# Moving background steps of a scan kernel by one or two scans, and clearing its padded images one at a time from a row of zeros

## The chip, the core and the metric

The kernel runs on one core of one Trainium2 chip. The metric is the device time of one execution in microseconds. A core has TensorE (PE, matmuls into PSUM), VectorE (DVE), ScalarE (ACT), GpSimd (POOL) and SyncE (SP), which here issues all DMAs. Each engine takes its instructions in program order and waits on semaphores for the others.

## What is computed

Eight images of 64 channels and 128 x 128 pixels, in float32, go one after the other through an adaptive filter and a block with two bidirectional state-space layers:

```python
# layer 0: a 3x3 filter with weights of its own for every pixel
h = leaky(conv3x3(x, w1)); w_lp = softmax(conv1x1(h, w2))      # 9 weights a pixel
x = x + sum_k shift_k(x) * (delta_k - w_lp_k)
# layer 1, on each image
x_norm = layernorm(x); seq = layernorm(tokens(x_norm)); res = seq    # 16384 tokens
for i in range(2):
    xz = rmsnorm(seq) @ in_proj                                 # x and z, 128 channels
    seq = seq + (mamba(x, z, forward) + mamba(x, z, backward)) @ out_proj
x_mamba = conv3x3(rmsnorm(seq), resconv) + res
x = x + depthwise3x3(conv1x1(x_norm)) * x_mamba
g1, g2 = split(depthwise3x3(conv1x1(layernorm(x), ffn_in)))     # 2 x 170 channels
x = x + conv1x1(gelu(g1) * g2, ffn_out)

# mamba, one direction
xc = silu(causal_conv1d(x)); dt_r, Bm, Cm = xc @ xproj
dt = softplus(dt_r @ dtproj + bias)
h[t] = exp(dt[t] * A) * h[t-1] + dt[t] * xc[t] * Bm[t]          # 128 channels x 16 states
y = (sum_n h * Cm + D * xc) * silu(z)
```

## The kernel before

**Scans.** The recurrence runs on DVE as a scan instruction along 1024 tokens, with 128 of the 128 x 16 (channel, state) pairs on the partitions. So a chunk of 1024 tokens takes 16 scans. An image has 16 chunks, two layers and two directions, 1024 scans; eight images have 8192. For scan `u` of a chunk ACT makes the decay `w` = exp(dt A) in one of two PSUM buffers (`decay`, L993), POOL makes the drive `bu` for two scans at once (`drive`, L985, three buffers), DVE scans (L1011, or L1013 in the backward direction), DVE (L1035) or POOL (L1032) multiplies by C (`product`), ACT keeps the last state (`keep`, L1025), and PE sums over the states (`collect`, L1051).

**The order of the work** is written out by hand. Nothing is issued at once: `at(time, phase, fn)` puts a step into a table, with the number of the scan beside which it is to be issued as its time and one of six phases in that scan (FEED, SCAN, MID, PROD, DECAY, REST). At the end the table is sorted and issued; that is the order of each engine's queue. The scheduler adds no order of its own, only the waits. Times below 0 come ahead of the first scan. Steps of the same time and phase stand in the order in which they were put in: the chunks' first, then image by image those of the front, of mix and of FFN.

**A chunk** prepares itself over the 32 scans ahead of its own (`Chunk.plan`): load of normed tokens, convolution, silu at -21, dt at -18 and -17 (`step`, L904), softplus at -14, B and C at -16, the store of dt to DRAM (`store_dt`, L938), then `dtx` on POOL (L941), which overwrites dt by dt * xc and so must wait for that store, the store of du, and the loads that spread both over the states (L952, L963). The second direction of a layer adds at its end, in the next chunk's scans, output projection, residual and rmsnorm: `means` on PE (L399), `means_out` on ACT (L405), `root` on POOL (L408, a power of -0.5), `spread` back over the channels on PE (L414), `normed` on DVE (L1097).

**Background.** Beside the scans of one image run, spread over the table: the *front* of the next image (layer 0, layer norms, the pointwise part of the depthwise branch; 16 pieces of 1024 pixels, one every 24 scans; `hidden` L442, `hidden_out` L446, `weighted` L498, `scaled` L523, `third_norm` L555), and of the image before *mix* (16 pieces, one every 13 scans: two 3x3 convolutions on PE, L638, `add_h` L651, `times` on DVE L658, `plus` on POOL L661, a layer norm) and *FFN* (16 pieces, one every 24 scans: three groups of convolutions on PE, L740 and L746; `first_out` L753; `gelus` on ACT, L757 and L759; `rest_times` L762; `times` L765; `project`; `add`; `store`). The front of the first image runs mostly ahead of the first scan; mix and FFN of the last image end after the last scan.

**PSUM** tiles that matter: chunk steps share one bank ("mm"), background steps two ("acc" and "bg"), the decays have two buffers ("w"). A step that needs one of these waits until the last reader of the tile before is through.

**Images in DRAM.** The 3x3 convolutions read windows out of five padded images (`x_img`, `xm_img`, `xn_img`, two `dw_img`), 64 rows of 131 x 130 floats each, whose rims must be zero. Before, ahead of all background, one tile of 64 x 17030 zeros is filled by DVE (L335) and stored into each of the five (L337); then pad columns of three token arrays are stored (L339, L340). `copy_x` (L618) copies an image of x into `x_img` in 16 pieces.

**SP** issues some 25,700 DMAs, all on one hardware queue; an issue that waits holds all behind it.

Of the kernel before, what the change touches and what calls it, by code (L numbers as in the profile page):

```python
# [8 lines left out]
F32 = mybir.dt.float32  # L9
# [7 lines left out]
C = 64  # L17
# [22 lines left out]
FRONT_STEP, MIX_STEP, FFN_STEP = 24, 13, 24  # L40
FRONT_AT, MIX_AT, FFN_AT = 594, 992, 1204

SILU, SOFTPLUS, GELU = 11, 18, 11

FIRST_FRONT_AT = -198
LAST_MIX_STEP, LAST_MIX_AT, LAST_FFN_STEP, LAST_FFN_AT = 16, 826, 12, 1084
# [9 lines left out]
def kernel(ctx: ExitStack, tc: tile.TileContext, a: dict, out: bass.AP):  # L56
# [20 lines left out]
    def dram(shape, name):  # L77
        return dramp.tile(shape, F32, tag=name, name=name + "_dram")


# [234 lines left out]

    def image(name):

        return dram([C, PW * PW + PW], name)

    def pixels(img):  # L320
        return img[:, 0 : PW * PW].rearrange("c (r w) -> c r w", w=PW)

    x_img, xm_img, xn_img = image("x"), image("xm"), image("xn")
    dw_img = [image(f"dw{i}") for i in range(2)]
    x1_dram = [dram([NCH, P, N], f"x1{i}") for i in range(2)]

# [5 lines left out]
    yf_dram = dram([NT, DI, T], "yf")  # L332
    with tc.tile_pool(name="zeros", bufs=1) as zp:
        zero = zp.tile([C, PW * PW + PW], F32, tag="zero", name="zero")
        nc.vector.memset(zero, 0.0)  # L335
        for img in (x_img, xm_img, xn_img, *dw_img):
            nc.sync.dma_start(img, zero)  # L337
        for t in (*hn0_dram, hn1_dram):
            nc.sync.dma_start(t[:, 0:PAD], zero[:, 0:PAD])  # L339
            nc.sync.dma_start(t[:, PAD + NT * T :], zero[:, 0:PAD])  # L340

# [85 lines left out]
    class Front:  # L427
# [134 lines left out]
        def plan(self, a):  # L562
# [3 lines left out]
            for i in range(3):  # L566
                at(b + 1 + i, REST, self.hidden, i)
            at(b + 4, DECAY, self.hidden_out)
            at(b + 21, REST, self.logits)
# [58 lines left out]
    class Mix(Front):  # L628
# [40 lines left out]
        def plan(self, a):  # L669
            n1 = self.n1  # L670
            at(a - 5, REST, self.load_conv, dw_img[self.p], "dww")
            at(a - 4, REST, self.load_conv, xm_img, "xmw")
            at(a - 1, REST, self.load_h)
            for i in range(3):
                at(a + i, REST, self.conv, 0, "dww", i)
                at(a + 3 + i, REST, self.conv, 1, "xmw", i)
            at(a + 3, DECAY, self.branch_out)
            at(a + 2, REST, self.load_x1)
            at(a + 5, REST, self.add_h)
            at(a + 7, DECAY, self.times)  # L680
            at(a + 7, REST, self.plus)
            at(a + 9, REST, self.store_x2)
            at(a + 9, REST, self.centered, bg_tile, "x1")
            at(a + 10, DECAY, self.centered_out)
            at(a + 11, REST, lambda: n1.means(bg_tile, self.sq))
            at(a + 12, DECAY, n1.means_out)
            at(a + 12, REST, n1.root)
            at(a + 15, REST, n1.spread, bg_tile)
            at(a + 16, DECAY, self.scaled, n1)
            at(a + 16, DECAY, self.norm)  # L690
            at(a + 16, REST, self.store_rows, xn_img, "hc")

# [6 lines left out]
    class Ffn:  # L699
# [54 lines left out]

        def gelus(self):
            for h in range(2):
                nc.scalar.activation(self.ga[h], self.ga[h], AF.Gelu)  # L757
            self.gt = tmp("gt")
            nc.scalar.activation(self.gt, self.rest[0], AF.Gelu)  # L759

# [31 lines left out]
        def plan(self, a):  # L792
            early = 12 if self.alone else 0
            at(a - 4 - early, REST, self.load, 0)
            at(a - 3 - early, REST, self.load, 1)

            if self.alone:
                groups = ((0, 0, self.first_out, 2), (3, 2, None, 0), (6, 1, self.times, 9))
                gelus, out = 5, 12
            else:  # L800
                groups = ((0, 0, self.first_out, 5), (6, 2, None, 0), (13, 1, self.times, 18))
                gelus, out = GELU, 20
            for t, g, end, to in groups:
                for i in range(4):
                    at(a + t + (0 if self.alone else i), REST, self.conv, g, i)
                for h in range(2 if end else 0):
                    at(a + to, DECAY, end, h)
            at(a + gelus, REST, self.gelus)
            at(a + gelus + 2, PROD, self.rest_times)
            at(a + out - 5, REST, self.load_x2)  # L810
            at(a + out, REST, self.project)
            at(a + out + 2, DECAY, self.add)
            at(a + out + 2, REST, self.store)
# [15 lines left out]
    class Chunk:  # L829
# [282 lines left out]
        def plan(self):  # L1112
# [17 lines left out]
            at(b - 14, REST, self.store_bc)  # L1130
            at(b - 12, REST, self.store_dt)
            at(b - 11, FEED, self.dtx)
# [37 lines left out]
            at(b + 12, FEED, lambda: n.means(mm_tile, self.sq))  # L1170
            at(b + 12, DECAY, n.means_out)
            at(b + 13, REST, n.root)
            at(b + 17, FEED, n.spread, mm_tile)
# [6 lines left out]
    for i, c in enumerate(chunks):  # L1180
        c.prev = chunks[i - 1] if i else None
        c.plan()
    for b in range(B):
        a, last = IMAGE * b, b == B - 1
# [36 lines left out]
```

## Time and profile before

| | |
|---|---|
| median of three runs | 30239.16 us (30228.46 to 30248.67) |
| the profiled execution | 30193.53 us; its span 30191.6 us |
| busy in the span | PE 24336.3, DVE 27115.8, ACT 18589.4, POOL 27650.2 us |
| first scan starts, last scan ends | 680.5 us, 29577.9 us |
| DMA | 6617 MB, 219 GB/s over the span |
| one scan, L1011 w | 2345 ns, 2677 of them |
| one product on DVE (L1035), on POOL (L1032) | 1225 ns, 2358 ns |
| one drive for two scans on POOL (L985) | 4534 ns |
| one decay on ACT (L993) | 1118 ns |

In the profile's lines a group is named by line, engine, operation and out<-in with the program's tile names. A wait is written as the waiting engine and instruction, an arrow, and what ended the wait. "SPq" is SP's issue of a DMA; the DMA itself lands later. In a timeline the columns are start in us, duration in us, engine, line, operation and tiles, how many instructions are merged, and in brackets the idle time of the engine before it with what ended it. A PE of which the profile says that it is busy needn't be at its peak.

### The profile page before, as it was taken

The numbers are of one execution on the slowest core, as the hardware profiler recorded it, in microseconds if no ns is written. First come the engines' busy times: TensorE is split into PE (matmuls) and PEld (weight loads), VectorE is DVE, ScalarE is ACT, GpSimd is POOL, SyncE is SP. The second block draws the span as 40 slices with busy tenths as digits, with TensorE's granted clock in tenths as the row PEclk, the third lists the DMA queues.
The fourth block names the chain that finished last, engine by engine and source line by source line (L and its number), as shares of the span: only waits on it lengthen the run. The fifth ranks groups of instructions, "written<-read, shape, count | busy, mean of one in ns | idle before, by whom it ended". The sixth has DMA issues, their size and how long they took to land. (4 is left out here: it accounts for less than half of the span.)

```text
span 30191.6 us, 307698 instructions
## 1 busy us (share of the span) xinstructions
PE 24336.3 (81%) x96344; PEld 8057.2 (27%) x96344; DVE 27115.8 (90%) x17258; ACT 18589.4 (62%) x28316; POOL 27650.2 (92%) x8732
## 2 busy tenths in 40 slices
PE   6766888878888788887888788887888878888589
PEld 2211232223222232222322223222232223322123
DVE  2999999999899998999999999999999999999992
ACT  2666666666666665666666666666666666666661
POOL 1999999999999999999999999999999999999991
PEclk8877889989899888988989889898899988999789
DMA  3676676766777667776777767677677766767672
GB/s 92 211 237 217 220 230 227 238 213 221 229 232 233 214 222 229 234 232 213 228 228 234 225 215 229 228 237 224 216 227 231 237 217 223 231 229 233 215 237 76
DMA packets 2488415, 6617.27 MB, mean 219 GB/s; under 512 B 417862, under 2 KB 680342, under 8 KB 2483830
## 3 DMA queue, kind: packets, MB, share of 16 engines
q1 hardware_dynamic: 2486774, 6597.59, 67.3%
q8 instruction: 761, 12.47, 0.2%
q14 instruction: 880, 7.21, 0.1%
HBM read 5363.40 MB, written 1266.10 MB: 220 GB/s over the span
## 5 line engine op out<-in xcount | busy, mean ns | idle before, releaser
L985 POOL TENSOR_TENSOR bu<-dup,bp 128x2048 f32<-128x2048 f32 x4096 | 18558.9, 4534 | 215.1 <-DVE w L1011 74.1
L993 ACT ACTIVATE w<-dtp,a_neg 128x1024 f32<-128x1024 f32 x8192 | 9158.4, 1118 | 394.7 <-DVE hs L1011 170.4
L1035 DVE TENSOR_TENSOR hs<-w,cp 128x1024 f32<-128x1024 f32 x5360 | 6565.0, 1225 | 333.8 <-DMA cp<-bc_dram 111.3
L1032 POOL TENSOR_TENSOR hs<-hs,cp 128x1024 f32<-128x1024 f32 x2832 | 6679.1, 2358 | 131.7 <-ACT state L1025 88.4
L1011 DVE TENSOR_TENSOR_SCAN w<-w,state,bu 128x1024 f32<-128x1024 f32 x2677 | 6278.0, 2345 | 297.3 <-ACT w L993 296.7
L1013 DVE TENSOR_TENSOR_SCAN w<-w,state,bu 128x1024 f32<-128x1024 f32 x2683 | 6289.9, 2344 | 262.1 <-ACT w L993 261.9
L1051 PE MATMUL y<-hs,sel_y 128*32 128x512 f32 x32768 | 5182.2, 705 | 103.0 <-POOL hs L1032 100.9
L1025 ACT COPY state<-w 128x1 f32<-128x1 f32 x5360 | 835.2, 156 | 5403.4 <-DVE hs L1035 5355.9
L1013 DVE TENSOR_TENSOR_SCAN hs<-w,state,bu 128x1024 f32<-128x1024 f32 x1413 | 3310.4, 2343 | 260.5 <-ACT state L1025 95.2
L1011 DVE TENSOR_TENSOR_SCAN hs<-w,state,bu 128x1024 f32<-128x1024 f32 x1419 | 3324.3, 2343 | 113.2 <-ACT w L993 54.8
L1044 PE MATMUL y<-xc,dskip 128*64 128x512 f32 x4096 | 1609.4, 853 | 1574.3 <-ACT yv L1068 1117.7
L863 PE MATMUL xp<-hn,wx 128*128 128x512 f32 x4096 | 2280.2, 684 | 719.3 <-ACT xc L869 603.5
L740 PE MATMUL fp<-fw,bgw 128*128 128x512 f32 (+1 forms) x6144 | 2288.4, 627 | 129.9 <-ACT ga L753 67.7
L408 POOL TENSOR_TENSOR r<-r,neg_half 128x8 f32<-128x8 f32 x768 | 1258.2, 1642 | 569.1 <-ACT r L405 494.7
L1051 PEld LDWEIGHTS y<-hs,sel_y 128*32 128x32 f32 x32768 | 751.7, 118 | 3801.2 <-issue 2601.8
L941 POOL TENSOR_TENSOR dt<-dt,xc 128x1024 f32<-128x1024 f32 x512 | 1208.6, 2361 | 568.9 <-DMA dt_dram<-dt 504.4
L1025 ACT COPY state<-hs 128x1 f32<-128x1 f32 x2832 | 538.5, 190 | 1701.2 <-DVE hs L1013 886.4
L904 PE MATMUL dp<-xc,wdt 128*128 128x512 f32 x2048 | 1229.1, 684 | 432.8 <-ACT dt L911 401.0
L746 PE MATMUL fp<-fw,bgw 64*128 64x512 f32 (+1 forms) x6144 | 1511.3, 612 | 0.0
L993 ACT ACT_TABLE_LOAD x1134 | 1454.9, 1283 | 20.6 <-DMA dtp<-dt_dram 0.6
L504 PE MATMUL acc<-t,ident 128*128 128x512 f32 x2304 | 1370.3, 679 | 0.0
L414 PE MATMUL rb<-ident,r 128*64 128x128 f32 x12288 | 959.3, 302 | 461.9 <-ACT state L1025 226.2
(184 smaller groups left out, 26678.6 us busy)
## 6 DMA issues: line engine op xcount, KB each, us to landing
bp<-bc_dram SPq DMA_DIRECT2D x4096, 256.0 KB, 3.8
dup<-du_dram SPq DMA_DIRECT2D x4096, 256.0 KB, 5.0
dtp<-dt_dram SPq DMA_DIRECT2D x4096, 256.0 KB, 5.1
cp<-bc_dram SPq DMA_DIRECT2D x4096, 256.0 KB, 4.8
hn<-hn_dram SPq DMA_DIRECT2D x1024, 256.5 KB, 4.4
dt_dram<-dt SPq DMA_DIRECT2D x512, 512.0 KB, 4.5
du_dram<-dt SPq DMA_DIRECT2D x512, 512.0 KB, 2.6
yf_dram<-yv SPq DMA_DIRECT2D x512, 256.0 KB, 3.5
```

The costliest lines, as they stand in the source:

```text
L740: nc.tensor.matmul(o, wpair[:, i, g, m], self.win[h][:, i : i + ROWS, 0:W], start=(i == 0), stop=False)
L746: nc.tensor.matmul(o, wlast[rows, i, g, m], self.win[h][rows, i : i + ROWS, lo : W + lo], start=False, stop=(i == 2),)
L863: nc.tensor.matmul(self.xp[h], wx[:, self.l, self.d, i, :], self.hn2[:, s.start + 2 * i : s.stop + 2 * i], start=(i == 0), stop=(i == 1),)
L985: nc.gpsimd.tensor_tensor(bu, self.dup[self.pairs[k][1]], self.over_pair("bp", k), ALU.mult)
L993: nc.scalar.activation(w, self.dtp[gp][:, i, :], AF.Exp, scale=a_neg[:, self.l, self.d, g, j : j + 1])
L1011: nc.vector.tensor_tensor_scan(to, w, bu, s0, ALU.mult, ALU.add)
L1013: nc.vector.tensor_tensor_scan(to[:, ::-1], w[:, ::-1], bu[:, ::-1], s0, ALU.mult, ALU.add)
L1025: nc.scalar.copy(self.column(u), h[:, T - 1 : T] if self.d == 0 else h[:, 0:1])
L1032: nc.gpsimd.tensor_tensor(hs, hs, c, ALU.mult)
L1035: nc.vector.tensor_tensor(hs, w, c, ALU.mult)
L1044: nc.tensor.matmul(self.y[C * h : C * h + C, :], dskip[:, self.l, self.d, C * gp : C * gp + C], self.xc[:, s], start=True, stop=False,)
L1051: nc.tensor.matmul(self.y[lo : lo + 32, :], sel_y, hs[:, i, s], start=False, stop=(k % 4 == 3))
```

## The change

- Five images are no longer cleared from a tile of 64 x 17030 zeros ahead of everything. A constant row of 130 zeros on 64 partitions is filled, and `clear` stores it 131 times over into one image with one DMA. `x_img` is cleared first of all, ahead of the loads of weights; `dw_img[0]` at the start of the first front (step -199), `xm_img` at step 64, `xn_img` at 128, `dw_img[1]` at 192, each behind the chunks' and ahead of the background's steps of its time and phase.
- The front starts one scan earlier (593 for 594, -199 for -198), and `hidden_out` stands two scans later in it.
- In mix, `times`, `plus` and all that follows come one scan later.
- In FFN, the gelu of the rest group is issued first of three, its product `rest_times` comes a scan earlier (in phase DECAY of +12 instead of PROD of +13), the third group of convolutions and its `times` one scan later, and the projection one scan earlier.
- In the chunks, the store of dt is issued one scan earlier, and `means_out` and `root` of the closing norm one scan later.

No arithmetic changes. The number of instructions is the same on each engine, apart from waits: 25,719 DMAs as before. Which products POOL takes stays as it was.

```diff
-FRONT_AT, MIX_AT, FFN_AT = 594, 992, 1204
+FRONT_AT, MIX_AT, FFN_AT = 593, 992, 1204
-FIRST_FRONT_AT = -198
+FIRST_FRONT_AT = -199
...
+    def clear(img):
+        nc.sync.dma_start(
+            img.rearrange("c (r w) -> c r w", w=PW),
+            zero.rearrange("c (o w) -> c o w", o=1).to_broadcast([C, PW + 1, PW]),
+        )
+
+    x_img, xm_img, xn_img = image("x"), image("xm"), image("xn")
+    dw_img = [image(f"dw{i}") for i in range(2)]
+    zero = const([C, PW], "zero")
+    nc.vector.memset(zero, 0.0)
+    clear(x_img)
...
-    with tc.tile_pool(name="zeros", bufs=1) as zp:
-        zero = zp.tile([C, PW * PW + PW], F32, tag="zero", name="zero")
-        nc.vector.memset(zero, 0.0)
-        for img in (x_img, xm_img, xn_img, *dw_img):
-            nc.sync.dma_start(img, zero)
-        for t in (*hn0_dram, hn1_dram):
-            nc.sync.dma_start(t[:, 0:PAD], zero[:, 0:PAD])
-            nc.sync.dma_start(t[:, PAD + NT * T :], zero[:, 0:PAD])
+    for t in (*hn0_dram, hn1_dram):
+        nc.sync.dma_start(t[:, 0:PAD], zero[:, 0:PAD])
+        nc.sync.dma_start(t[:, PAD + NT * T :], zero[:, 0:PAD])
...
-            at(b + 4, DECAY, self.hidden_out)
+            at(b + 6, DECAY, self.hidden_out)
...
-            at(a + 7, DECAY, self.times)
-            at(a + 7, REST, self.plus)
-            at(a + 9, REST, self.store_x2)
-            at(a + 9, REST, self.centered, bg_tile, "x1")
-            at(a + 10, DECAY, self.centered_out)
...
+            at(a + 8, DECAY, self.times)
+            at(a + 8, REST, self.plus)
+            at(a + 10, REST, self.store_x2)
+            at(a + 10, REST, self.centered, bg_tile, "x1")
+            at(a + 11, DECAY, self.centered_out)
...
         def gelus(self):
+            self.gt = tmp("gt")
+            nc.scalar.activation(self.gt, self.rest[0], AF.Gelu)
             for h in range(2):
                 nc.scalar.activation(self.ga[h], self.ga[h], AF.Gelu)
-            self.gt = tmp("gt")
-            nc.scalar.activation(self.gt, self.rest[0], AF.Gelu)
...
-                groups = ((0, 0, self.first_out, 5), (6, 2, None, 0), (13, 1, self.times, 18))
-                gelus, out = GELU, 20
+                groups = ((0, 0, self.first_out, 5), (6, 2, None, 0), (14, 1, self.times, 19))
+                gelus, out = GELU, 19
...
-            at(a + gelus + 2, PROD, self.rest_times)
+            at(a + gelus + 1, DECAY, self.rest_times)
...
-            at(b - 12, REST, self.store_dt)
+            at(b - 13, REST, self.store_dt)
...
-            at(b + 12, DECAY, n.means_out)
-            at(b + 13, REST, n.root)
+            at(b + 13, DECAY, n.means_out)
+            at(b + 14, REST, n.root)
...
+    for t, img in ((FIRST_FRONT_AT, dw_img[0]), (64, xm_img), (128, xn_img), (192, dw_img[1])):
+        at(t, REST, clear, img)
```

(In mix, all later steps of `plan` move by the same one scan.)

More of the change, by code (lines that the diff above doesn't have):

```diff
@@ L78, in dram, with image, pixels @@
         return dramp.tile(shape, F32, tag=name, name=name + "_dram")
+    def image(name):
+        return dram([C, PW * PW + PW], name)
+    def pixels(img):
+        return img[:, 0 : PW * PW].rearrange("c (r w) -> c r w", w=PW)
+    def clear(img):
[8 more added lines that the diff above has]
+    clear(x_img)
     ident = const([P, P], "ident")
@@ L313 @@
                 nc.vector.tensor_scalar(dskip[:, l, d, :], ident, dp, None, ALU.mult)
[L316 to L324, printed above, removed]
     x1_dram = [dram([NCH, P, N], f"x1{i}") for i in range(2)]
@@ L679, in plan @@
             at(a + 5, REST, self.add_h)
-            at(a + 7, DECAY, self.times)
-            at(a + 7, REST, self.plus)
-            at(a + 9, REST, self.store_x2)
-            at(a + 9, REST, self.centered, bg_tile, "x1")
-            at(a + 10, DECAY, self.centered_out)
[L685 to L691, printed above, removed]
+            at(a + 8, DECAY, self.times)
[3 more added lines that the diff above has]
+            at(a + 11, DECAY, self.centered_out)
+            at(a + 12, REST, lambda: n1.means(bg_tile, self.sq))
+            at(a + 13, DECAY, n1.means_out)
+            at(a + 13, REST, n1.root)
+            at(a + 16, REST, n1.spread, bg_tile)
+            at(a + 17, DECAY, self.scaled, n1)
+            at(a + 17, DECAY, self.norm)
+            at(a + 17, REST, self.store_rows, xn_img, "hc")
     def plan_mix(b, a, step):
```

## The prediction

> **What bounds the kernel now.** I read the page first, then the stretches of time, then what VectorE (DVE) and GpSimd (POOL) wait for while scans run, then the timeline of the opening.
>
> ```profile
> span 30191.6 us, 307698 instructions
> ## 1 busy us (share of the span) xinstructions
> PE 24336.3 (81%) x96344; PEld 8057.2 (27%) x96344; DVE 27115.8 (90%) x17258; ACT 18589.4 (62%) x28316; POOL 27650.2 (92%) x8732
> ```
>
> Two engines are full at once. The stretches part the span in three: the opening, 0 to 680.5 us (the first scan), in which DVE works only some 135 us; 680 to 29578 us, the 8192 scans, with DVE busy 26940 and POOL 27575 of 28898 us; then a tail of 613 us in which PE is busy 576. One step of the plan (one scan) is 28898 / 8192 = 3.53 us. So three kinds of time can be won: the opening, DVE's idle 1958 us among the scans (6.8%), and POOL's idle 1323 us as far as DVE waits for POOL. PE's tail stays.
>
> The opening, by its timeline:
>
> ```profile
> 102.34 14.25 DVE L335 MEMSET zero<- 64x17030 f32 x1 [3.70 <-issue]
> 116.66 0.66 SPq L337 DMA_DIRECT2D x_dram<-zero  x1
> ...
> 139.86 0.45 SPq L340 DMA_DIRECT2D hn_dram<-zero  x1
> 161.16 0.45 SPq L339 DMA_DIRECT2D hn_dram<-zero  x1
> 182.43 0.45 SPq L340 DMA_DIRECT2D hn_dram<-zero  x1
> 203.74 49.73 SPq L618 DMA_DIRECT2D x_dram<-in_x  x16
> 253.52 2.90 SPq L382 DMA_DIRECT2D xa<-x_dram  x2
> ...
> 269.00 9.82 PE L442 MATMUL hp<-xa,bgw 128*64 128x512 f32 x18 [170.78 <-DMA xa<-x_dram]
> ```
>
> The weights are ready at 98.6 us; the first matmul of the front starts at 269.0, after 170.78 us of waiting. Between lie five images' zeros. The issues at 139.86, 161.16, 182.43 and 203.74 are 21.3 us apart: each stands until one more image (4.36 MB) is written, since an issue on SP waits for the DMA eight before it.
>
> What DVE, then POOL, waits for from 750 to 29500 us (us in total, times, longest):
>
> ```profile
> DVE w L1011 <- ACT w L993: 296.2, 262, 3.9
> DVE w L1013 <- ACT w L993: 261.9, 185, 4.9
> DVE dwv L658 <- PE cv L651: 208.9, 87, 4.7
> DVE hc L523 <- PE rb L414: 187.1, 129, 4.1
> DVE hn L1097 <- PE rb L414: 123.5, 95, 7.9
> ...
> DVE hn L555 <- PE rb L414: 102.9, 69, 5.3
> ```
> ```profile
> POOL dt L941 <- DMA dt_dram<-dt: 504.4, 212, 9.8
> POOL r L408 <- ACT r L405: 278.9, 160, 4.4
> ```
>
> POOL's longest wait, for the store of dt, is in part a wait of an engine that is ahead: DVE stood only 35.4 us for POOL's bu in that stretch.
>
> [...] pad stores of 12 bytes a row, issued behind the images, landed after 94.3 us. [...] from 680 to 29500 us packets of 4096 bytes took 188 ns on average, those of 4104 bytes 279. [...] The trace has the load (1283 ns, 1.28 us) and 0.02 us behind it [...].
>
> **The change, part by part.** Plus is a loss.
>
> 1. *Opening.* Gone from the path: the 14.25 us memset and the wait for five images. Added: one clear of x at the very start, 64 x 131 = 8384 pieces of 520 bytes. The nearest row is the 512-byte packets into these images, 38 ns: 8384 x 38 ns / 16 engines = 20 us. The upper bound adds the 91 ns that 4104 bytes cost over 4096: 129 ns, 68 us. I take 25 us. It isn't free: SP's eighth DMA after it waits for it, so instead of at 15.2 us the first weights (w1n) are issued at about 25 + 17 issues x 0.62 = 36 us, and the whole preparation is some 20 us later. SP is through with its weights at 84 us now, so at 104; six pad stores make 107. From the second copy of x (225.1 us) to the first matmul now pass 43.9 us; so the matmul starts at 151 instead of 269: **-118** (-138 if the preparation isn't held, -75 at 68 us a clear). The clear of dw0 lies after the second load of xa, in today's time 7.6 us ahead of the matmul; the load of xb behind it is used 26 us after that. Some 28 us are covered, so 0; at 68 us it costs 40.
>
> 2. *The three clears at steps 64, 128, 192.* Each closes the queue for 25 us = 7 steps, in the first front. The store of dt lands then at about step 8 of the chunk instead of 5, and POOL stands at L941 some 12 us, of which its lead over the scans takes a part: 8 us each, **+24** (+5 to +160).
>
> 3. *Mix, from `times` on one step later.* PE is late with the convolution; L658 waits 2.4 us on average, at most 4.7; a step is 3.53. Nearly all 209 us of it go. Next late are the decay w from ScalarE (ACT; 1.4 us a chunk in these stretches) and rb. DVE is the fuller engine's follower here (idle 5.4 us of a chunk's 56.9, POOL 2.95), so I take two thirds: **-135** (-70 to -209). `plus`, the stores and the norm move along at the same distances. In the tail nothing moves, as no scan sets the pace.
>
> 4. *A PSUM clash that goes.* Last front chunk and first mix chunk both ask for the one "bg" tile at step 1001: rb (L414) stood 4.60 us for ACT's hc (L520) at 11441 us, and DVE 5.16 us for it at L555. The front now asks at 1000, mix at 1002: seven images x 5.2 = 36, I take **-30** (-36 to 0).
>
> 5. *Front one step earlier otherwise.* The three `hidden` groups leave PE at chunk steps 10 to 12 instead of 11 to 13, so dp at 14 finds PE free (ACT waits 518 us for dp in all); other meetings turn for the worse. **-30** (-120 to +60). `hidden_out` two steps later frees ACT's queue in front of first_norm: in the opening both were ready within 1 us (376.1 and 377.1 us), so 0.
>
> 6. *Store of dt one step earlier.* In the 188 chunks where POOL waits over 1 us at L941, the store was issued a median 3.3 us after softplus had ended, with SP busy otherwise; now it is next. Some 400 of 504 us of POOL's wait go. But who waits for L941 is PE's y for 23.9 us, rb for 3.0 and DVE for 0.4; with a share of DVE's waits for rb I take **-50** (-150 to +20).
>
> 7. *Means and root of the chunk's norm one step later.* ACT's r comes clear of the silu burst; POOL's 279 us at L408 shrink, but two steps remain to the use. **-10** (-40 to +40).
>
> 8. *FFN.* rest_times (L762) goes from step +13 to +12, the gelu it needs (0.58 us) from third to first. Over the 112 gelus beside scans the table load ends 1.35 us (median) after DVE is through with step +12, so the gelu's result comes 1.9 to 2.2 us after; DVE stands 2.1 us and works 0.69 ahead of scan +13. Now, rest_times follows scan +13, and scan +14 then stands 1.43 us for its decay. New: 2.1 + 0.69 + 3.55 (scan and product) = 6.4 us to scan +14; now 5.7. That is +0.7 x 100 = +70 (0 to +258). The convolution at +14 then no longer stands for rest_times (51 us on PE), but in every second FFN chunk its last part meets dp at chunk step 14. Together **+70**.
>
> Sum: -118 + 24 - 135 - 30 - 30 - 50 - 10 + 70 = -279. The profiled execution took 30193.53 us, its span 30191.6 and 1.9 around it; it would take 29914. It lies 46 us (0.15%) below the median of the runs, 30239.16, so the median falls to **29960 us** (0.9% less). One measurement tells 0.2%, about 60 us, from no change.
>
> **Rivals.** (a) *The gelu's wait isn't given back:* DVE stands 2.3 us at each of 112 rest_times and scan +14 is as late as ever: +258 instead of +70, and the steady gains are gone: 30239 - 279 + 188 = 30148. For it: the burst on ACT (three gelus, two loads, 4.3 us) isn't shorter. Against: DVE would have stood 1.43 us anyway. (b) *POOL is the bound* (it is busier, 95.4% against 93.2%): its waits at L941 and L408 then count, 300 instead of 60: 29720. Against: DVE hardly waits for bu. (c) *SP is held by the early store.* It now stands for softplus in nearly every chunk; queued behind it are load_hn, which PE needs four steps later, and the windows. If that makes each of 512 chunks 0.8 us later, +410, and part 6 falls away: 30239 - 229 + 410 = 30420, slower. It decides from 0.57 us a chunk. Against: a load lands in 4.4 us and has 14. (d) *The clears don't do what they say:* at 68 us each, parts 1 and 2 give +125 instead of -94: 30180.
>
> **Chances.** Forecast 0.53, (a) 0.18, (b) 0.13, (c) 0.08, (d) 0.08. The forecast's own range is 29850 to 30070. The range of 8 in 10 reaches to (a) and most of the way to (b): 29750 to 30160. Faster by over 0.2%: nearly all of the forecast, (b), most of (a), half of (d): 0.81; within 0.2%: 0.10; slower 0.09.
>
> **What would show it.** First hp matmul near 150 us and first scan near 562 instead of 680.5; L658's wait for cv below 60 us; L555's wait at mix start gone; POOL's L941 below 150; DVE idle ahead of L762 about 200 us beside scans, and less ahead of scan +14; three stalls of 5 to 15 us at the steps 64, 128 and 192. I am wrong if the first matmul stays above 200 us, or if DVE's waits among the scans (1958 us) don't shrink by at least 100.

## The result, and the profile after

| | before | after |
|---|---|---|
| median, us | 30234.28 (30228.46 to 30248.67) | 29968.85 (29955.96 to 29988.73) |
| ratio | | 0.9912, 95% interval 0.9895 to 0.9929 |
| the profiled execution, us | 30193.53 | 29956.31 |
| first hp matmul, us | 269.0 | 160.6 |
| first scan starts, us | 680.5 | 579.7 |
| from the first scan's start to the last one's end, us | 28897.4 | 28757.6 |
| from there to the end, us | 613.7 | 617.1 |

The time fell by 265 us (0.88%); 29960 had been forecast. Two profiled executions differ by 237 us, since the one of before lay 41 us under its median and the one of after 13: of these 237 the opening gives 101 and the scans 140, and the tail takes 3.

I call the third last row "the scans" below. It is worked out from the starts of DVE's scans in the trace, and so are the lengths of chunks (from the first scan of one chunk to the first of the next).

**The page.** Both engines did the same work as before in less time:

```profile
span 29954.4 us, 307972 instructions
## 1 busy us (share of the span) xinstructions
PE 24257.7 (81%) x96344; PEld 8093.1 (27%) x96344; DVE 27086.6 (90%) x17258; ACT 18533.8 (62%) x28316; POOL 27661.8 (92%) x8732
```

**The opening**, SP's timeline first, then PE's and DVE's:

```profile
1.38 0.57 SPq L89 DMA_DIRECT2D x_dram<-zero  x1
2.00 23.91 SPq L160 DMA_DIRECT2D v_norm_w<-in_L_conv_norm_w  x1
...
41.97 0.31 SPq L216 DMA_DIRECT2D w1n<-in_L_conv_w  x1
...
112.74 31.03 SPq L624 DMA_DIRECT2D x_dram<-in_x  x16
143.88 3.00 SPq L388 DMA_DIRECT2D xa<-x_dram  x2
...
153.87 0.55 SPq L89 DMA_DIRECT2D dw_dram<-zero  x1
```
```profile
160.61 10.44 PE L448 MATMUL hp<-xa,bgw 128*64 128x512 f32 x18 [35.49 <-DMA xa<-x_dram]
```
```profile
192.98 0.69 DVE L504 TENSOR_TENSOR t<-xb,wb 128x512 f32<-128x512 f32 x1 [16.91 <-DMA xa<-x_dram]
```

The wait of PE shrank from 170.78 to 35.49 us. But the clear of x holds SP at the very next issue, for 23.91 us, and the first weights (w1n) go out at 42.0 us instead of 15.2. (The eighth issue behind the clear stands once more, until the clear has landed at 32.7 us, as the eighth behind the first image of zeros did before, until 139.86 us; so SP would have stood that long without the first stand.) The last line is the clear of dw0 at work: the first `weighted` comes 32.4 us after the first hp matmul instead of 26.1.

**The clear at step 64**, on SP, then PE, ACT, DVE and POOL:

```profile
812.88 0.60 SPq L89 DMA_DIRECT2D xm_dram<-zero  x1
816.28 22.15 SPq L517 DMA_DIRECT2D x_dram<-x  x1
838.53 1.21 SPq L566 DMA_DIRECT2D hn_dram<-hn  x2
839.79 1.04 SPq L940 DMA_DIRECT2D bc_dram<-bc  x2
840.93 0.38 SPq L944 DMA_DIRECT2D dt_dram<-dt  x1
841.41 5.49 SPq L859 DMA_DIRECT2D hn<-hn_dram  x2
```
```profile
850.59 3.75 PE L869 MATMUL xp<-hn,wx 128*128 128x512 f32 x4 [19.28 <-DMA hn<-hn_dram]
```
```profile
854.37 0.69 ACT L875 ACTIVATE xc<-xp,cbias 128x512 f32<-128x512 f32 x1 [16.43 <-PE xp L869]
```
```profile
858.57 2.35 DVE L1017 TENSOR_TENSOR_SCAN hs<-w,state,bu 128x1024 f32<-128x1024 f32 x1 [16.21 <-ACT w L999]
```
```profile
848.86 2.35 POOL L947 TENSOR_TENSOR dt<-dt,xc 128x1024 f32<-128x1024 f32 x1 [19.09 <-DMA dt_dram<-dt]
```

Read them from the top down. SP stands 22 us, so the load of hn for a chunk to come is issued only at 841.4, and its second half only at 846.4, when the clear has landed; PE stands at its convolution for hn, ACT at the eviction xc of that convolution, the decay w is queued behind xc on ACT, and DVE's scan stands for w. Beside this runs a second path: the store of dt was held too, POOL stands 19.09 us for it, and its drive for the same scan is ready at 855.7 us, only 2.8 ahead of w (at step 192 the two are 0.5 us apart). So without the delay of hn this scan would still have stood about 13 us, an estimate from these two times. The chunks of the three clears took 75.1, 73.9 and 69.8 us instead of 55.3, 55.3 and 50.5, together 57.7 more.

**What DVE, then POOL, waits for**, 700 to 29250 us (the window shown of before was 750 to 29500; each leaves out some 70 us of scans at the start and 80 at the end):

```profile
DVE w L1017 <- ACT w L999: 340.3, 298, 3.2
DVE w L1019 <- ACT w L999: 313.5, 193, 3.2
DVE hc L529 <- PE rb L420: 209.9, 112, 4.5
DVE gt L768 <- ACT gt L763: 171.8, 107, 2.2
DVE hn L1103 <- PE rb L420: 133.3, 78, 3.7
DVE hn L561 <- PE rb L420: 123.4, 63, 14.4
```
```profile
POOL bu L991 <- DVE w L1019: 421.4, 274, 2.6
POOL dt L947 <- DMA dt_dram<-dt: 221.4, 118, 20.4
POOL hs L1038 <- ACT state L1031: 131.0, 149, 3.9
POOL bu L991 <- DVE w L1017: 116.3, 90, 2.9
POOL r L414 <- ACT r L411: 101.6, 101, 2.6
```

The wait of `times` for cv (208.9 us before) has gone from the list, the wait of `rest_times` for the gelu is new. POOL waits less for the store of dt and for r, and much longer for DVE to leave bu's buffers (537.7 instead of 146.3 us): POOL is ahead of DVE.

### The profile page after: what moved, and what is told of

It reads as the page before. It is cut to its first block, busy times and chain, and to the rows that moved or that the text cites. A ratio compares the mean times of both kernels' runs of the same rounds, so it can differ in the third digit from the quotient of the medians.

```text
span 29954.4 us, 307972 instructions
## 1 busy us (share of the span) xinstructions
PE 24257.7 (81%) x96344; PEld 8093.1 (27%) x96344; DVE 27086.6 (90%) x17258; ACT 18533.8 (62%) x28316; POOL 27661.8 (92%) x8732
## 3 DMA queue, kind: packets, MB, share of 16 engines
q1 hardware_dynamic: 2528054, 6597.59, 68.4%
## 5 line engine op out<-in xcount | busy, mean ns | idle before, releaser
L1038 POOL TENSOR_TENSOR hs<-hs,cp 128x1024 f32<-128x1024 f32 x2832 | 6685.3, 2361 | 197.9 <-ACT state L1031 133.3
L1041 DVE TENSOR_TENSOR hs<-w,cp 128x1024 f32<-128x1024 f32 x5360 | 6564.9, 1225 | 310.9 <-DMA cp<-bc_dram 77.6
L1017 DVE TENSOR_TENSOR_SCAN w<-w,state,bu 128x1024 f32<-128x1024 f32 x2677 | 6280.9, 2346 | 346.5 <-ACT w L999 345.9
L1019 DVE TENSOR_TENSOR_SCAN w<-w,state,bu 128x1024 f32<-128x1024 f32 x2683 | 6291.0, 2345 | 314.1 <-ACT w L999 313.5
L1017 DVE TENSOR_TENSOR_SCAN hs<-w,state,bu 128x1024 f32<-128x1024 f32 x1419 | 3321.3, 2341 | 86.4 <-ACT w L999 36.9
L1019 DVE TENSOR_TENSOR_SCAN hs<-w,state,bu 128x1024 f32<-128x1024 f32 x1413 | 3307.7, 2341 | 52.8 <-ACT w L999 34.7
L746 PE MATMUL fp<-fw,bgw 128*128 128x512 f32 (+1 forms) x6144 | 2353.9, 638 | 64.7 <-ACT ga L759 63.5
L875 ACT ACTIVATE xc<-xp,cbias 128x512 f32<-128x512 f32 x1024 | 697.2, 681 | 1415.1 <-PE xp L869 1414.7
```

What stands on the lines that cost most here:

```text
L746: nc.tensor.matmul(o, wpair[:, i, g, m], self.win[h][:, i : i + ROWS, 0:W], start=(i == 0), stop=False)
L1017: nc.vector.tensor_tensor_scan(to, w, bu, s0, ALU.mult, ALU.add)
L1019: nc.vector.tensor_tensor_scan(to[:, ::-1], w[:, ::-1], bu[:, ::-1], s0, ALU.mult, ALU.add)
L1038: nc.gpsimd.tensor_tensor(hs, hs, c, ALU.mult)
L1041: nc.vector.tensor_tensor(hs, w, c, ALU.mult)
```

## The experiments

Each run is built on the changed kernel, but for the first, which is built on the one before. The kernel before ran on the same chip beside each group of four; its median was 30239 us beside runs 1 to 4, 30224 beside 5 to 8 and 30275 beside 9 to 12. So medians of different groups are comparable to some 40 us only, and I give the scans too, which come from one profiled execution each. The executions of a run lie up to 60 us apart. "Against after" is the difference from 29968.85, and from 28757.6.

| run | median, us | ratio to before, 95% | against after | scans | against after |
|---|---|---|---|---|---|
| before + clears alone | 30166.11 | 0.9978 (0.9969 to 0.9987) | | 28958.3 | |
| FFN back | 29916.83 | 0.9897 (0.9884 to 0.9911) | -52 | 28689.8 | -68 |
| store of dt back | 30109.86 | 0.9962 (0.9948 to 0.9976) | +141 | 28911.0 | +153 |
| mix back | 30068.49 | 0.9944 (0.9932 to 0.9957) | +100 | 28852.6 | +95 |
| front and hidden_out back | 29888.60 | 0.9887 (0.9872 to 0.9902) | -80 | 28713.0 | -45 |
| norm's steps back | 29958.96 | 0.9911 (0.9896 to 0.9926) | -10 | 28754.2 | -3 |
| rest_times alone back | 29938.98 | 0.9903 (0.9888 to 0.9918) | -30 | 28747.1 | -11 |
| clears in eighths | 29876.10 | 0.9881 (0.9865 to 0.9898) | -93 | 28693.3 | -64 |
| own du, store of dt back | 29910.60 | 0.9885 (0.9870 to 0.9900) | -58 | 28705.4 | -52 |
| own du | 29947.62 | 0.9895 (0.9881 to 0.9910) | -21 | 28722.3 | -35 |
| hidden_out alone back | 29887.77 | 0.9875 (0.9858 to 0.9891) | -81 | 28677.1 | -81 |
| eighths, FFN and front back | 29763.47 | 0.9834 (0.9819 to 0.9849) | -205 | 28582.5 | -175 |

**1. The clears alone.** The kernel before with the part of the diff from `image` and `clear` to the pad stores, and the line that plans the four clears; no step is moved.

> The kernel before with the new clears alone (one row of zeros, x cleared at the start, dw0 at -198, xm, xn and dw1 at 64, 128 and 192); every step of mix, FFN, front, norm and the store of dt where it was. Theory: the clears bring the whole of the opening's change and the whole loss of image 0, nothing else: first scan near 580 us instead of 680.5 (-101), the chunks of steps 64, 128 and 192 longer by 19.5 us each (+58), all other chunks within 1 us of before. Sum -43, median near 30190. Rival 1 (the forecast's own sum, clears nearly free): -94, 30140. Rival 2 (the moved steps are what made the opening shorter or the three chunks longer): the opening or these chunks differ by more than 10 us from the changed kernel's.

Measured: 73 us less than the kernel before; the interval, 39 to 94 us less, hardly tells the theory from rival 1, but the trace does. The first hp matmul is at 160.8 us, as in the changed kernel. The chunks of the three clears take 76.1, 72.6 and 72.9 us and image 0 is 64 us longer than before; the other seven together are 3 us shorter. So the clears alone make the jump to 160 us and image 0's loss; rivals 1 and 2 fall. The first scan came at 585.6 us.

**2. FFN as before.**

```diff
-            self.gt = tmp("gt")
-            nc.scalar.activation(self.gt, self.rest[0], AF.Gelu)
             for h in range(2):
                 nc.scalar.activation(self.ga[h], self.ga[h], AF.Gelu)
+            self.gt = tmp("gt")
+            nc.scalar.activation(self.gt, self.rest[0], AF.Gelu)
...
-                groups = ((0, 0, self.first_out, 5), (6, 2, None, 0), (14, 1, self.times, 19))
-                gelus, out = GELU, 19
+                groups = ((0, 0, self.first_out, 5), (6, 2, None, 0), (13, 1, self.times, 18))
+                gelus, out = GELU, 20
...
-            at(a + gelus + 1, DECAY, self.rest_times)
+            at(a + gelus + 2, PROD, self.rest_times)
```

> The changed kernel with FFN as before: the third gelu last again, rest_times at +13 behind the product, the second group of the convolution at 13, times at 18, the projection at 20. Forecast (the FFN edit costs 70): this kernel is 70 faster than the changed one, 29899. Theory from the trace (the stretch of FFN became 7.2 us an image shorter, and the edit did that): 7 x 7.2 = 50 slower, 30020. Rival: the 7.2 us come from the store of dt or the norm's steps, which are in every chunk; then within 15 us of 29969. The rival (a) of the forecast (the gelu's wait isn't given back) would make this 250 faster.

Measured: 52 us faster than the changed kernel, in the scans 68. So the edit cost about what the forecast had said (70), and my reading of the trace was wrong: the stretch of FFN had become shorter through the other parts, which are in every chunk, and the edit had taken some of it back. DVE no longer waits for the gelu, and waits for the next scan's inputs instead:

```profile
DVE hs L1019 <- issue: 116.8, 77, 1.8
DVE hs L1019 <- ACT state L1031: 87.0, 53, 2.4
```

In the changed kernel the second of these lines is 11.0 us and the first isn't there. By the step of the FFN piece, the first stands at scan +14 (121 us, forward scans included), where the forecast had it, and most of the second at scan +18 (76 us). Run 7, which moves `rest_times` alone, has the first and not the second. So of the 172 us that DVE stood for the gelu about 120 were given back at scan +14; the 76 at +18 go with another of FFN's moves. Against them stand the waits for the decays (L1019's wait for w is 261.1 us instead of 313.5, L1017's 325.2 instead of 340.3), above all at scan +23 of the piece: 75 us in the changed kernel, 8 here.

**3. Store of dt at -12 again.**

```diff
-            at(b - 13, REST, self.store_dt)
+            at(b - 12, REST, self.store_dt)
```

> The changed kernel with the store of dt at -12 again. Forecast (the early store wins 50): 30019. Theory from the trace: POOL's wait for this store only moved to a wait for bu's buffers, which DVE's scans set free, so POOL isn't the bound: within 20 us of 29969, while POOL's wait for the stored dt is back near 500 us and its waits for w fall from 538 to some 250. Rival (SP was held by the early store): 50 to 200 faster.

Measured: 141 us slower. My theory fell, and the forecast's 50 was too small by almost three times. What PE waits for in this run, then in the changed kernel:

```profile
PE cp L521 <- POOL x L667: 214.9, 63, 8.0
...
PE rb L420 <- POOL r L414: 187.4, 89, 5.0
PE y L1057 <- POOL hs L1038: 113.9, 74, 4.9
```
```profile
PE cp L521 <- POOL x L667: 147.7, 50, 6.3
...
PE rb L420 <- POOL r L414: 117.0, 60, 5.0
PE y L1057 <- POOL hs L1038: 27.0, 27, 3.4
```

POOL stands 644.0 us for the store of dt instead of 221.4. What is queued behind it on POOL (products, roots, mix's sum) comes later, so PE stands for POOL 516 us instead of 292, and DVE's waits for rb and wb, which PE makes, grow with it: L529 from 209.9 to 249.8, L561 from 123.4 to 147.6, L504 from 37.6 to 60.5 (L1103 falls from 133.3 to 113.8). These make some 70 of the 153 us. Another 32 are waits of the product for a load of cp (L1041, 109.3 instead of 77.6 us) and 21 waits of scans for POOL's bu itself. SP too stands longer for POOL's product at the store of du (L951, 3635.5 us instead of 2774.8), so the loads queued behind it are a way by which the delay can reach cp; no run takes that apart.

**4. Mix as before:** `times` and `plus` at 7, store and `centered` at 9, and so on to 16.

> The changed kernel with mix as before (times at 7, plus at 7, the stores and norm one step earlier again), all else as changed. Forecast: -135 was this part's gain, so 135 slower, 30104; DVE's wait for cv at times is back near 200 us, 1.9 us a chunk. Theory from the trace: the mix stretch (steps 0 to 176 of an image) loses the 16.9 us an image it won, 7 x 16.9 = 118 slower, 30087. The chunk of step 992 stays near 60 us, since the front keeps its earlier step and asks for the bg tile at 1000 against the mix's 1001. Rival: the gain of the mix stretch came from the store of dt and the norm's steps: less than 60 slower.

Measured: 100 us slower. The steps 0 to 176 lose 20.2 us an image (141 in seven), other stretches win a part of it back. The wait is back at its length of before:

```profile
DVE dwv L664 <- PE cv L657: 214.8, 85, 4.7
```

The chunk of step 992 stays at 59.8 us (68.7 before), as the theory had it.

**5. Front and hidden_out as before.**

```diff
-FRONT_AT, MIX_AT, FFN_AT = 593, 992, 1204
+FRONT_AT, MIX_AT, FFN_AT = 594, 992, 1204
-FIRST_FRONT_AT = -199
+FIRST_FRONT_AT = -198
...
-            at(b + 6, DECAY, self.hidden_out)
+            at(b + 4, DECAY, self.hidden_out)
```

> The changed kernel with the front at 594 and -198 again and hidden_out at 4 again; mix keeps its later step, so the two still ask for the bg tile one step apart (1001 and 1002). Forecast: the earlier front won 30 beside the tile's clash, so 30 slower, 29999. Theory from the runs so far: clears -73, FFN +52, store of dt -141 and mix -100 already make -262 of the -265, and the chunk of step 992 won 8.4 us in seven images (59), which each of the two moves does alone; so the front's other meetings and the norm's steps must cost some 50 together: up to 50 faster, 29920, with the chunk of 992 still near 60 us. If that chunk goes back to 68.6 us, the tile needs more than one step between the two.

Measured: 80 us faster by the medians, 45 in the scans (image 2 alone is 19 us longer than in the changed kernel and image 3 is 2, the others are shorter; the execution profiled lay 26 us above the run's median). The chunk of 992 takes 61.4 us: one step between the two is enough for the tile. The front as changed costs time. Run 11 tells which half of it.

**6. The norm's steps as before:** `means_out` at 12, the root at 13.

> The changed kernel with means_out at 12 and the root at 13 again. Forecast: the later steps win 10, so 29979, with POOL's wait for r back from 102 to some 280 us. Theory from the runs so far: POOL isn't the bound, but PE stands for POOL's r and DVE for PE, as with the store of dt; so POOL's longer wait could cost as much per us as there: 178 us of wait instead of 440 gives some 50 slower, 30020. Rival (the two later steps make rb later than DVE needs it): up to 40 faster, with DVE's wait for rb at L1103 below 134 us.

Measured: 10 us less by the medians, 3 in the scans: no difference that shows. POOL's wait for r is 145.8 us, not 280, so most of what went at L408 had gone through other parts; the theory of 50 fell. The first scan of this run came at 601.7 us, 22 later than in the changed kernel's profile, although nothing of the opening was changed. The stretch from 300 to 440 us, first in the changed kernel, then here (after the engines' busy times come granted clock, DMA share and GB/s):

```profile
300.00:440.00 140.00, 114.56 (x426) 52.43 (x426) 25.61 (x46) 24.96 (x55) 17.46 (x18) 0.83 0.14 38
```
```profile
300.00:440.00 140.00, 118.65 (x387) 52.20 (x385) 24.23 (x44) 21.95 (x49) 15.25 (x17) 0.74 0.12 34
```

At a granted clock of 0.74 instead of 0.83 PE does 387 matmuls instead of 426 there. So beyond the first hp matmul the opening scatters from one execution to the next: from there to the first scan the fourteen profiles take 411 us (before, at a clock of 0.81) to 447 us (run 9, at 0.76).

**7. rest_times alone as before** (at `gelus + 2`, phase PROD).

> The changed kernel with rest_times alone at +13 behind the product again; the gelu's order, the second group of the convolution at 14, times and projection at 19 stay as changed. Theory (the forecast's step 8: DVE stands 2.1 us for the gelu at +12, and gets only part of it back): the whole loss of FFN sits here, 52 faster, 29917, and DVE's wait for the gelu (171.8 us) is below 20. Rival (the later second group and the earlier projection cost it): within 15 of 29969.

Measured: 30 us faster by the medians, 11 in the scans; its executions (29902 to 29962) reach into those of the changed kernel, so the gain itself isn't shown. The wait for the gelu is gone from the list of DVE's waits, and 118 of its 172 us are back at scan +14. L1019's wait for w stays at 313.0 us here and is 261.1 in run 2: the wait at scan +23 is still 73 us. So what more run 2 wins goes with the order of the gelus (issued at +11), the later group of convolutions and its `times` (at 14 and 19) or the earlier projection (at 19). By the place of the wait it is more likely the later ones; none was tried alone.

**8. The clears in eighths.**

```diff
-    def clear(img):
+    def clear(img, i, n):
+        r0, r1 = (PW + 1) * i // n, (PW + 1) * (i + 1) // n
         nc.sync.dma_start(
-            img.rearrange("c (r w) -> c r w", w=PW),
-            zero.rearrange("c (o w) -> c o w", o=1).to_broadcast([C, PW + 1, PW]),
+            img.rearrange("c (r w) -> c r w", w=PW)[:, r0:r1, :],
+            zero.rearrange("c (o w) -> c o w", o=1).to_broadcast([C, r1 - r0, PW]),
         )
...
-    for t, img in ((FIRST_FRONT_AT, dw_img[0]), (64, xm_img), (128, xn_img), (192, dw_img[1])):
-        at(t, REST, clear, img)
+    for t, d, img in ((FIRST_FRONT_AT, 3, dw_img[0]), (64, 8, xm_img), (128, 8, xn_img), (192, 8, dw_img[1])):
+        for i in range(8):
+            at(t + d * i, REST, clear, img, i, 8)
```

The eighths of x are issued one ahead of each of the four pairs of loads in FFN's weights and of each of the four loads of `cw`.

> The changed kernel with each clear cut into eight parts by rows: x's among the loads of the weights, dw0's every third step from -199, those of xm, xn and dw1 every eighth step from 64 to 248. The bytes and pieces are the same. Theory (a clear costs because it closes the one queue for 28 us at a time, and its parts, 3.5 us each, fit under the loads' lead): the chunks of steps 64, 128 and 192 go back to 55.3, 55.3 and 50.5 us, no other chunk grows by more than 1 us (-58), and the opening gains up to 27 since the preparation is no longer held (first scan 555 to 580): 29890 to 29915. Rival (it is the DMA engines' time, 28 us a clear, whatever its cut): 29969 within 15, the loss spread over the chunks of steps 64 to 255.

Measured: 93 us faster by the medians, 64 in the scans. The three chunks take 56.3, 57.4 and 51.1 us, image 0 is 53.7 us shorter, and the first hp matmul starts at 146.7 us. SP's timeline around the same place:

```profile
805.38 0.60 SPq L90 DMA_DIRECT2D xm_dram<-zero  x1
808.78 0.33 SPq L519 DMA_DIRECT2D x_dram<-x  x1
809.55 1.14 SPq L568 DMA_DIRECT2D hn_dram<-hn  x2
```

The store behind the clear is issued in 0.33 instead of 22.15 us. The same zeros in the same pieces cost next to nothing in parts of some 4 us each, an estimate (an eighth of the 31 to 35 us that a whole clear took to land): shorter than the lead of the loads behind them (before, the load of hn at this step was issued at 918.3 us, 12.7 ahead of the convolution that takes it). The rival (the DMA engines' time counts) falls. In the changed kernel the store of dt issued at 840.93 us, behind the whole clear, took 7.9 us to land (median of that kernel 3.1) and landed 2.4 us after the clear. But most of the delay arose before that, in the issues. Behind the eighth, the load of hn is issued 10.8 us after the clear instead of 28.5, and in the three chunks PE does not wait for a load of hn, nor POOL's product for a store of dt.

**9 and 10. A tile of its own for dtx**, with the store of dt at -12 (9) and at -13 (10):

```diff
-            nc.gpsimd.tensor_tensor(self.dt, self.dt, self.xc, ALU.mult)
+            self.du = wk.tile([P, T], F32, tag="du", name="du", bufs=1)
+            nc.gpsimd.tensor_tensor(self.du, self.dt, self.xc, ALU.mult)
...
-            nc.sync.dma_start(self.du_d, self.dt)
+            nc.sync.dma_start(self.du_d, self.du)
...
-        return wk.tile([P, N], F32, tag="tmp", name=name, bufs=14)
+        return wk.tile([P, N], F32, tag="tmp", name=name, bufs=13)
```

> The changed kernel with the store of dt at -12 again, but the product of dt and x (dtx on POOL) goes into a tile of its own instead of over dt, so POOL no longer has to wait until dt is stored; the pool of small tiles has 13 buffers instead of 14 to make room. Theory (the early store won its 141 us because POOL's wait for the stored dt reached DVE over POOL's products and roots, PE's y and rb): the wait at the product is gone and with it the loss, so 29969 or less, and PE's waits for POOL's hs, r and x are at most the 292 us of the changed kernel instead of 517. Rival (the order on the queue is what counts: the store one step earlier lets the loads behind it start earlier): near 30110, as with the store at -12 before.

> The same tile of its own (and 13 small buffers), with the store of dt at -13 as in the changed kernel. Theory: the place of the store no longer matters, this run and the one before lie within 20 us of each other, some 0 to 40 below 29969 (POOL's last 221 us at this wait go too). Rival (the queue's order): some 140 faster than the run before. If the 13 buffers cost anything, both show it.

Measured: 29911 and 29948 us. With the store at -12 the tile takes 199 us off run 3 (206 in the scans), and POOL's product no longer waits for the store of dt. PE's waits for POOL in run 9:

```profile
PE cp L521 <- POOL x L667: 147.5, 49, 6.3
PE rb L420 <- POOL r L414: 104.9, 58, 4.9
PE y L1058 <- POOL hs L1039: 22.2, 23, 2.7
```

They add up to 275 us, as in the changed kernel (292) and not as in run 3 (516). So what the early store won, it won by ending POOL's wait for it. The rival, by which the earlier place on the queue itself is the gain, falls: with the wait gone, the early store is 37 us (17 in the scans) the slower of the two, not 140 the faster. Run 9 also answers for the clears: though POOL waits for no store there, and the drive is ready 22 us ahead of w, the scan in the chunk of step 64 stands 16.4 us for w, and the three chunks take 71.5, 68.4 and 67.6 us. So the path of hn is enough by itself.

**11. hidden_out alone as before** (at `b + 4`); the front stays at 593 and -199.

> The changed kernel with hidden_out at 4 again, the front itself staying at 593 and -199. Theory: hidden_out at 6 sets free the accumulator of PE only at the chunk step at which pointwise of the chunk before asks for it (24 + 6 = 30), so PE stands 4.0 us for ha in 103 chunks (411.8 us in all), which the forecast held for free; this wait goes (below 20 us), and the run is 40 to 80 faster, like the run with the whole front put back (29889). Rival (it is the front's one step that costs): within 20 of 29969, though the wait is gone.

Measured: 81 us faster, in the medians and in the scans. The costliest group of pointwise in the changed kernel, then in this run (busy, mean ns, idle of PE ahead of it):

```profile
L538 PE MATMUL dwp<-hc,bgw 128*128 128x512 f32 x256 | 211.9, 922 | 441.0 <-ACT ha L453 440.1 <-ACT hc L533 0.9
```
```profile
L538 PE MATMUL dwp<-hc,bgw 128*128 128x512 f32 x256 | 151.2, 674 | 23.3 <-ACT hc L533 23.3
```

DVE's waits for the decays w fall from 654 to 510 us (272.4 and 237.7); 63 us of that come back as longer waits for rb and wb. Only the runs with this edit, 5 and 12 among them, have lost PE's wait, so the changed kernel lost some 80 us by `hidden_out`. Whether the front's one step by itself is a gain isn't shown: run 5 differs from this one by it alone, and its scans are 36 us longer, but the medians lie within 1 us.

**12. What the runs point to:** eighths of run 8, FFN of run 2, front of run 5.

> What the runs point to: the changed kernel with the clears in eight parts each, FFN as before and the front at 594, -198 with hidden_out at 4; kept are the small clears, mix one step later, the store of dt one step earlier and the norm's steps. If the parts add up as measured one at a time (-93, -52, -80 by medians; -69, -48, -41 by the profiled executions): 29745 to 29810. If front and FFN share a wait (both let PE stand): up to 29850.

Measured: 29763 us, 0.9834 of the kernel before. Its scans are 175 us shorter than the changed kernel's; 64 + 68 + 45 = 177 had been found one at a time. In the scans the parts add up.

## Why the prediction was right, and which of its steps failed

The forecast of 29960 is met within 9 us. Between the two profiled executions it is off by more: 279 us were forecast and 237 came. And it is a sum of eight terms, of which several were wrong in both directions. In the scans, each part as its undoing showed it (rows 1, 2 and 4 otherwise, see below):

| part | forecast, us | runs, us |
|---|---|---|
| 1 opening | -118 | -101 in the profile (first hp matmul -108) |
| 2 three clears | +24 | +61 |
| 3 mix | -135 | -95 |
| 4 the bg tile's clash | -30 | -60 |
| 5 front one step earlier | -30 | -36 (medians: -1) |
| 5 hidden_out | 0 | +81 |
| 6 store of dt | -50 | -153 |
| 7 the norm's steps | -10 | +3 |
| 8 FFN | +70 | +68 |

The scans' rows, 2 to 8, add up to -131, and the scans became 140 us shorter; so little is left over. Each row compares one profiled execution with another, and a row under some 40 us is not told from nothing. Row 2 is run 1 against before. Row 4 is the chunk of step 992 in seven images (68.7 to 60.1 us), which neither run 4 nor run 5 gives back, as each of the two moves is enough; no run undoes both, so it may hold something of other parts.

Of the signs that the forecast named, the early hp matmul came, L658's wait for cv went, and DVE's idle time among the scans fell by 127 us (1957.5 to 1830.3). The three stalls at the clears came at 14.4 to 16.2 us, against 5 to 15. Two signs did not come: POOL's wait for the store of dt stayed at 221 us, not below 150, and the wait of `third_norm` (L555, now L561) at the start of mix fell from 5.3 to 2.2 us an image and isn't gone.

*1, opening.* The mechanism is right, the size is off by 10 us up to the first hp matmul. "SP's eighth DMA after it waits for it" held; that the very next one stands 23.91 us too was not foreseen, and costs nothing on top here. The clear took 31.3 us to land, not 25, so w1n went out at 42.0 us, not 36. "Some 28 us are covered, so 0" for dw0's clear failed too: the first `weighted` lost 6 us. What follows scatters from one execution to the next (411 us at a granted clock of 0.81 before, 447 us at 0.76 in run 9): in the profiles of runs 1 to 7 and 9 to 11 the hp matmul came between 159 and 165 us and the first scan between 578.6 and 610.9. The profile of before (411 us from hp matmul to scan) and that of the changed kernel (419) both lie at the short end, so the 101 us hold for this pair and not for the medians.

*2, clears.* The term that was mis-sized. I followed the store of dt to POOL, "of which its lead over the scans takes a part", and found 8 us. That path was under-sized: POOL stood 19.0 to 20.4 us there, not 12, and its lead took only some 5 of them (its drive was ready 2.8 us before w at step 64 and 0.5 at step 192). And I left out a path as long, one place further down the same queue: the load of hn, to PE, to ACT's xc, to the decay w (the lines above), with a stall of 16.2 us; in run 9 it alone makes 16.4. Rival (c) had named hn as standing behind a held SP; I hadn't used it here.

*3, mix.* All of L658's wait went, as said. Two thirds of 209 us were assumed to stay won, and it was not quite half.

*4.* Right in kind; next to L555's wait, others of the same chunk shrank (L1097's from 6.0 to 1.5 us).

*5.* The sign of the sum is wrong. The front's step itself may do what was said, but its 36 us stand in the profiles alone. The error is "`hidden_out` two steps later frees ACT's queue ... so 0". I looked at the engine that does it and at the opening, and not at who waits for the tile that it sets free. At 6, in the period of 24, it falls on step 30 of an earlier piece, where `pointwise` asks for the same accumulator: PE stands 4.0 us in 103 pieces.

*6, store of dt.* Right in kind: from 700 to 29250 us POOL's wait fell from 486 to 221 us, of which 59 are at the three clears. The share was wrong: I read who waits directly for L941. What is queued behind it on POOL, and then on PE, carries the delay on to rb and wb, and some of it comes by bu and the loads of cp (run 3). This underestimate of 103 us and the 81 us missed in 5 nearly cancel; that the total fits is in part luck.

*7* is nothing. *8* is right in size, and in part of its mechanism: DVE's wait for the gelu came as said (171.8 us, 2.2 at most; about 200 were expected), and about 120 of it are given back at scan +14, which leaves some 50 of the "+0.7 x 100". But taking back `rest_times` alone won only 11 to 30 us (run 7). What the forecast doesn't have is an exchange at later steps: the changed kernel loses some 67 us at scan +23 to a late decay and wins 76 at scan +18. These go with the gelus' order, the convolution at 14, `times` at 19 or the projection at 19; which of these it is stays open, and so does how the 68 us are made up.

*Rivals.* (a) falls with run 2: not 258 but 52 to 68. (b) falls as the bound, since POOL now waits 538 us for DVE; but its thought, that POOL's waits count for more than DVE's list says, was right for part 6. (c) falls: the early store is the larger gain. A cost of its sign may be there in small, 17 to 37 us between runs 9 and 10; whether it is the load of hn that makes it isn't shown. (d) falls for the opening; 31 to 35 us a clear lie much nearer to 25 than to 68.

## What to carry to other kernels

Price a large transfer on a shared queue by every load and store behind it, and follow each to the engine that sets the pace: here two of them were late by nearly the same. Cut into parts shorter than their lead, the same bytes were all but free (164.7 us for the three chunks, 161.1 before). When a step moves, look up which buffer it sets free and who asks for that buffer at the new time, and ask it in the period of the loop, where, at a period of 24, +6 and +30 are the same moment. And a wait of an engine that isn't the bound is not priced by its direct waiters alone (in run 3 POOL stood 423 us longer for the store of dt, and the scans took 153 more): what stands behind it in order on that engine, and then on the next, counts too.

## What the runs showed of the hardware

A clear of 8384 pieces of 520 bytes took 31.3 us (x) and 35.1 us (the second dw) from issue to landing, where the trace has the landing, and the pieces 61 to 69 ns on average over the five clears, more than the 38 ns of 512-byte stores into the same images and less than the 129 ns of the forecast's upper price. No run tells whether their size or where they start makes the difference. The pieces of before, of 34060 bytes and 2663 ns on average, cleared an image in 21.3 us. The trace's answer on the clear's line:

```profile
DMA to landing us min/median/max: 31.3/33.2/35.1
```

SP does not only stand for a DMA eight places back, as until 32.7 us in the opening: the issue right behind such a clear itself stands 22 to 24 us (12.4 behind the first dw, where it comes 17 us later), at the start of the program too, where nothing eight places back exists. With an eighth of the pieces, the two issues behind the first part of x take 0.66 and 1.86 us.
